# A graph layer in one kernel: each row's diagonal block formed last and stored once, with degrees subtracted, and ten pieces of A kept on chip

## The chip, the core and the metric

The kernel runs on one core of a Trainium2 chip. The core has five engines that run side by side, each with its own queue of instructions: TensorE (PE; its weight loads are listed apart as PEld), VectorE (DVE), ScalarE (ACT), GpSimd (POOL) and SyncE (SP), which here only issues transfers. Sixteen DMA engines move data between device memory and SBUF; a transfer is issued from the queue of SP, ACT or POOL. TensorE writes into PSUM, from which the other engines read. The metric is the device time of one execution in microseconds (us), as the median of several runs. All times below are from one profiled execution unless they are said to be runs.

## What is computed

With B = 8 graphs that share one adjacency of N = 4096 nodes, and F = FO = 256 features:

```python
def _L0_gnn_ref(H, W, A):
    HW = jnp.einsum('bnf,fo->bno', H, W)
    A_norm = jax.nn.relu((A + A.T) * 0.5)
    D = jnp.sum(A_norm, axis=1)
    D_safe = jnp.where(D > 0, D, 1.0)
    d_inv_sqrt = jnp.where(D > 0, D_safe ** (-0.5), 0.0)
    DAD = d_inv_sqrt[:, None] * A_norm * d_inv_sqrt[None, :]
    L_norm = jnp.eye(N, dtype=H.dtype) - DAD
    out = jnp.einsum('nm,bmo->bno', L_norm, HW)
    return jax.nn.relu(out)

x = _layernorm(x + _L0_gnn_ref(x, L0_gnn_W, adj), axis=-1)
```

The inputs are `x` (8, 4096, 256), `adj` (4096, 4096) and the 256 x 256 weights, all float32.

## The kernel before

**Algebra.** With r = d_inv_sqrt and e the degrees (1 where a degree is 0), row n of L_norm times HW is -r[n] times the sum over m of (A_norm - diag(e))[n, m] * r[m] * HW[m]. So the kernel forms A = A_norm and subtracts e from its diagonal, forms G = r * HW, multiplies, and scales with minus_r at the end.

**Stage 1, up to 585 us.** A is formed in 512 x 512 blocks, 8 rows of blocks by 8. For row i the loop takes the diagonal block (i, i) first and then, for j = i+1 to 7, the pair (i, j) and (j, i). One pass of the inner loop is called a step. In a step:

- `load_adj` brings the one or two blocks (1 MB each, SP's queue, 4 buffers `adj`).
- `symmetrise` transposes a block on PE (L515, 16 records a block, four PSUM buffers of the tag "b0") and VectorE adds the untransposed block into `sym` (L519, 4 additions a block; `sym` has 3 buffers).
- `beside` holds other work for PE in that step: first `multiply` for groups that are ready, then `form` for one new group of 128 nodes. `quota` gives one group to each pair step and to the diagonal steps of rows 4 to 7, none to the diagonal steps of rows 0 to 3.
- `keep` applies the relu with the factor one half (ACT, L523), takes sums over 32 columns (DVE, L526), marks which are used (POOL, L527), adds them up into `part` (L531) and stores the block to `a_dram` (1 MB, ACT's queue, L532). For a diagonal block POOL also copies its four 128 x 128 pieces on the diagonal into `diag` (L537).

When the last pair of row i is done, `degrees(i)` works out the row's e, r and minus_r from `part` (L543 to L547; the power is POOL's). `lower_diagonal` then subtracts e from the four pieces in `diag` (VectorE, L555) and stores each over its place in `a_dram` (POOL's queue, L558, 64 KB), behind the store of the whole block. `release_all(i)` calls it, after it has scaled the row's "held" groups.

`form(m)` transposes x of group m (L615), copies it from PSUM (ACT, L616), multiplies with the weights (L626), and evicts the 1 MB of G with the factor r (L636) to `g_dram` (L641). Groups 0 to 21 are formed when their r is known. The ten groups 22 to 31 are formed early and unscaled, held in SBUF, and scaled in `release` (L649, L651). In both cases `fetch(m)` brings a strip, A's rows of the group by its first 128 columns (64 KB from `a_dram`, POOL's queue, L574, 10 buffers), and `multiply` adds strip times G to `lead`, four PSUM banks that hold output block 0 for the length of stage 1 (L584).

Between the steps, `run_due` does pieces of another job, the lists of used columns. Two of its tiles, `hot` and `mixed`, sit in a `sym` and an `adj` buffer for some steps. Its last piece in a turn, `collect`, multiplies into `pl` on PE (L449), and `index` reads that on VectorE (L463 to L479).

**Stage 2** gathers the used columns of A and rows of G with indirect transfers on POOL's queue (L1031, L1039) and multiplies them (L1254) for the other 31 output blocks; VectorE and ScalarE finish each block with the residual and the normalisation. It reads `a_dram`, so it starts when the last store has landed; `lead` of the ten held groups runs before it on PE.

**Order.** Each engine works its queue in order. The order is made when the program is built, by a scheduler that takes instructions roughly in the order of the code, weighed by when their inputs are ready, and pools decide which earlier tile a new one waits for. Stores on ACT's queue stand between ACT's own instructions and wait there.

Of the kernel before, what the change touches and what calls it, by code (L numbers as in the profile page):

```python
# [9 lines left out]
F32 = mybir.dt.float32  # L10
AF = mybir.ActivationFunctionType
ALU = mybir.AluOpType
# [55 lines left out]
def kernel(  # L68
# [40 lines left out]
    HOLD = 10  # L109
# [36 lines left out]
    ident = const.tile([P, P], F32, name="ident")  # L146
# [12 lines left out]
    a_dram = dram.tile([N + 1, N], F32, name="a_dram")  # L159
# [66 lines left out]
    own = const.tile([P, NE, 2], F32, name="own")  # L226
# [263 lines left out]
    with (  # L490
# [9 lines left out]
        }  # L500
        strips = holds.enter_context(tc.tile_pool(name="strips", bufs=10))

# [18 lines left out]

        def keep(i, j, sym, diag):
            nc.scalar.activation(sym, sym, AF.Relu, scale=0.5)  # L523
            rows = slice(i * A, (i + 1) * A)
            sums = stat1.tile([P, A, S // E], F32, tag="sums", name=f"sums_{i}_{j}", bufs=3)
            nc.vector.tensor_reduce(sums, sym.rearrange("p a (c q) -> p a c q", q=E), AX.X, ALU.add)  # L526
            ins = nc.gpsimd.tensor_scalar(  # L527
                uses[:, rows, j * S // E : (j + 1) * S // E], sums, 0.0, None, ALU.is_gt
            )
            flags.append(ins.ins)  # L530
            nc.vector.tensor_reduce(part[:, rows, j], sums, AX.X, ALU.add)  # L531
            nc.scalar.dma_start(  # L532
                a_dram[i * S : (i + 1) * S, j * S : (j + 1) * S].rearrange("(a p) s -> p a s", p=P), sym
            )
            if i == j:
                for a in range(A):
                    nc.gpsimd.tensor_copy(diag[:, a, :], sym[:, a, a * P : (a + 1) * P])  # L537

# [9 lines left out]

        def lower_diagonal(i, diag):
            ms = slice(i * A, (i + 1) * A)  # L550
            minus_e = stat1.tile([P, A], F32, tag="minus_e", name=f"minus_e_{i}")
            nc.vector.tensor_scalar(minus_e, e[:, ms], -1.0, None, ALU.mult)
            for a in range(A):
                m = i * A + a
                nc.vector.scalar_tensor_tensor(  # L555
                    diag[:, a, :], ident, minus_e[:, a : a + 1], diag[:, a, :], ALU.mult, ALU.add
                )
                nc.gpsimd.dma_start(  # L558
                    a_dram[m * P : (m + 1) * P, m * P : (m + 1) * P], diag[:, a, :]
                )  # L560

# [14 lines left out]
        def fetch(m):  # L576

            t = strips.tile([P, P], F32, tag="strip", name=f"strip_{m}")
            load(t, a_dram[m * P : (m + 1) * P, :P])
            return t  # L580
# [73 lines left out]

        diags = {}

        def release_all(i):
            for m in range(i * A, (i + 1) * A):
                if m in held:
                    release(m)  # L660
            lower_diagonal(i, diags.pop(i))

# [55 lines left out]
        for i in range(NS):  # L718
            diag = stat1.tile([P, A, P], F32, tag="diag", name=f"diag_{i}")
            for j in range(i, NS):  # L720
                tij = load_adj(i, j)
# [24 lines left out]
                for (rows, cols, _, _), sym in parts:  # L746
                    keep(rows, cols, sym, diag)
                    run_due()
            degrees(i)
            diags[i] = diag  # L750
            if i != NS - 2:
# [221 lines left out]
    with (  # L973
# [292 lines left out]
        for q, (u, step) in enumerate(steps):  # L1266
            new = q == 0 or steps[q - 1][0] != u
            if new:
                prepare(u)
                after(4, classify, u)  # L1270
                rows = [2 * u + 1 + b for b in range(2)] if q > 0 and blocks(u) == 2 else []
# [33 lines left out]
            for c in range(NC):  # L1305
                for op in step:
                    rows = slice(0, P) if op[1] is None else slice(op[1] * L, (op[1] + 1) * L)
                    cols = slice(op[3] * E, (op[3] + op[4]) * E)
# [82 lines left out]
```

## Time and profile before

| | |
|---|---|
| runs | 1518.41 us median of 3 (1517.39 to 1519.67) |
| the profiled execution | 1526.28 us, span 1524.6 us, mean granted clock of TensorE 0.976 |
| traffic | 540.52 MB, mean 355 GB/s |
| stage 1 | 0 to about 585 us: `lead` of the held groups ends, `py` begins |
| stage 2 | 585 to 1524.6 us |

How to read the rows. A row of the page's groups has the line, engine, operation, tiles with the last loop numbers left out, and the count; behind the first bar the busy time in us and the mean of one in ns, behind the second the idle time of the engine just before, with what ended it. A row of the timeline has start, length, engine, line and tiles, "x4" for four instructions in a row, and in brackets the wait before the first of them with what ended it. A row of the windows has the window, its length, busy time and count for PE, PEld, DVE, ACT and POOL, then the granted clock, the DMA share and GB/s. The chain of waits is followed back from the end: start, length, what it was. A matmul of float32 shows as two records, so a group's four products into `lead` are eight.

### The profile page before, as it was taken

To read this page: it belongs to the slowest core of one execution; us is meant where nothing else is said; L and a number is where in the kernel's file an instruction comes from. 1 tells how busy PE (TensorE), PEld (TensorE's weight loads), DVE (VectorE), ACT (ScalarE), POOL (GpSimd) and SP (SyncE) were. 2 spreads that over 40 slices of the span, in tenths; PEclk is the share of its full clock that TensorE was granted. 3 is DMA by queue.
4 is the path that set the end of the run, shared out by engine and by line. 5 is a ranking of instruction groups with operands and counts; after the bars stand their busy time and mean duration, and the time that the engine had idled before them with its cause. 6 is when DMAs were issued, how large, how long until landed. Compare 5 with 4: busy or idle time off the path is not lost.

```text
span 1524.6 us, 20569 instructions
## 1 busy us (share of the span) xinstructions
PE 1430.9 (94%) x6768; PEld 759.5 (50%) x6768; DVE 1028.0 (67%) x3010; ACT 369.3 (24%) x462; POOL 744.7 (49%) x1547
## 2 busy tenths in 40 slices
PE   7999988989999999989999989998999999989996
PEld 6777867777777753333333333332333333333332
DVE  5677569789597726074757676886799149879544
ACT  4555544544455430000000101010100010101102
POOL 3444010012133327556667565576476635756663
PEclk9999999989999999999999989999999999999998
DMA  9999999998999999888989899999899969998996
GB/s 349 364 371 387 405 364 363 386 362 329 393 358 326 371 418 362 337 320 328 358 304 371 288 396 348 356 383 413 294 382 358 412 206 372 364 347 299 405 396 236
DMA packets 215264, 540.52 MB, mean 355 GB/s; under 512 B 17750, under 2 KB 107526, under 8 KB 180838
## 3 DMA queue, kind: packets, MB, share of 16 engines
q0 software_dynamic: 53808, 281.94, 48.1%
q1 hardware_dynamic: 93200, 126.62, 23.9%
q10 hardware_dynamic: 68144, 130.58, 22.5%
q8 instruction: 56, 0.92, 0.2%
q14 instruction: 56, 0.46, 0.1%
HBM read 425.72 MB, written 136.34 MB: 369 GB/s over the span
## 4 chain that ended last, share of the span: by engine, by line
PE 64%; DVE 14%; DMA 14%; issue 3%; ACT 2%; POOL 1%; another core or an unknown queue 1%; ACTq 0%; DVEq 0%; POOLq 0%
PE py L1254 46%; PE pg L626 8%; DMA a_dram<-sym 7%; PE lead L584 5%; DVE sym L519 4%; DMA xin<-in_x_dram 4%; DMA g<-g_dram,gi 2%; PE xtr L615 2%; PE tr L515 2%; ACT sym L523 1%; DVE sums L526 1%; DVE stats L806 1%; DVE xr L797 1%; PE lists L449 1%; DVE xr L830 1%
## 5 line engine op out<-in xcount | busy, mean ns | idle before, releaser
L1254 PE MATMUL py<-g,ga 128*32 128x512 f32 (+4 forms) x2880 | 651.4, 604 | 16.3 <-issue 11.4
L1254 PEld LDWEIGHTS py<-g,ga 128*32 128x32 f32 (+4 forms) x2880 | 230.5, 138 | 408.3 <-issue 389.8
L1039 POOL DMA_INDIRECT g<-g_dram,gi x256 | 288.9, 1128 | 164.3 <-issue 74.3
L1031 POOL DMA_INDIRECT ga<-a_dram,ai x256 | 271.7, 1061 | 159.4 <-issue 59.9
L787 ACT ACTIVATE y<-py,minus_r 128x512 f32<-128x512 f32 x120 | 81.0, 687 | 824.7 <-PE py L1254 598.8
L1254 PE MATMUL py<-g_hub,gh 128*128 128x512 f32 x496 | 234.5, 614 | 13.5 <-DVE low L464 6.6
L626 PE MATMUL pg<-w_sb,xt 128*128 128x256 f32 x1024 | 231.7, 385 | 7.9 <-ACT xt L616 7.7
L626 PEld LDWEIGHTS pg<-w_sb,xt 128*128 128x128 f32 x1024 | 195.8, 194 | 35.5 <-ACT xt L616 8.7
L519 DVE TENSOR_TENSOR sym<-tr,adj 128x512 f32<-128x512 f32 x256 | 162.2, 683 | 60.6 <-PE tr L515 51.1
L526 DVE TENSOR_REDUCE sums<-sym 128x64 f32<-128x2048 f32 x64 | 145.5, 2279 | 64.4 <-ACT sym L523 64.4
L1254 PEld LDWEIGHTS py<-g_hub,gh 128*128 128x128 f32 x496 | 92.3, 194 | 142.3 <-issue 127.2
L527 POOL TENSOR_SCALAR uses<-sums 128x64 uint8<-128x64 f32 x64 | 26.7, 417 | 268.4 <-DVE sums L526 234.9
L515 PE MATMUL tr<-ident,adj 128*128 128x128 f32 x1024 | 137.7, 282 | 19.2 <-DVE sym L519 14.0
L523 ACT ACTIVATE sym<-sym 128x2048 f32<-128x2048 f32 x64 | 122.7, 1918 | 122.4 <-DVE sym L519 118.3
L515 PEld LDWEIGHTS tr<-ident,adj 128*128 128x128 f32 x1024 | 115.6, 143 | 50.4 <-DVE sym L519 31.5
L241 DVE TENSOR_TENSOR_SCAN incl_r<-carry,lists 128x32 f32<-128x32 bf16 x13 | 2.9, 220 | 164.9 <-PE lists L396 164.9
L428 DVE TENSOR_TENSOR hot<-iota_q,at 128x1024 bf16<-128x1024 f32 x64 | 74.6, 1219 | 33.9 <-ACT y L787 32.1
L797 DVE TENSOR_TENSOR xr<-xr,y 128x2048 f32<-128x2048 f32 x31 | 70.8, 2284 | 38.9 <-ACT y L787 34.3
L615 PE MATMUL xtr<-ident,xin 128*128 128x128 f32 x512 | 71.9, 291 | 18.9 <-DVE sym L519 9.8
L830 DVE TENSOR_SCALAR xr<-xr,mv,root 128x256 f32<-128x256 f32 x248 | 84.3, 412 | 1.1
L806 DVE BATCH_NORM_STATS2 stats<-xr 128x6 f32<-128x256 f32 x248 | 84.0, 412 | 1.1
L584 PE MATMUL lead<-gt,strip 128*128 128x512 f32 x176 | 82.4, 593 | 0.0
(164 smaller groups left out, 1038.4 us busy)
## 6 DMA issues: line engine op xcount, KB each, us to landing
adj<-in_adj_dram SPq DMA_DIRECT2D x64, 1024.0 KB
a_dram<-sym ACTq DMA_DIRECT2D x64, 1024.0 KB
out_dram<-xr SPq DMA_DIRECT2D x31, 1024.0 KB
xr<-in_x_dram ACTq DMA_DIRECT2D x28, 1024.0 KB
xin<-in_x_dram SPq DMA_DIRECT2D x44, 512.0 KB
g_dram<-gt ACTq DMA_DIRECT2D x22, 1024.0 KB
xin<-in_x_dram POOLq DMA_DIRECT2D x20, 512.0 KB
g_dram<-held ACTq DMA_DIRECT2D x10, 1024.0 KB
```

The lines of the kernel that those rows point to most:

```text
L515: ins = nc.tensor.transpose(pt[:, c * P : (c + 1) * P], tji[:, c, a * P : (a + 1) * P], ident)
L519: nc.vector.tensor_add(sym[:, a, :], pt, tij[:, a, :])
L523: nc.scalar.activation(sym, sym, AF.Relu, scale=0.5)
L526: nc.vector.tensor_reduce(sums, sym.rearrange("p a (c q) -> p a c q", q=E), AX.X, ALU.add)
L584: nc.tensor.matmul(lead[c], lhsT=strip, rhs=g[:, c * S : (c + 1) * S], start=not done, stop=len(done) == NB - 1, skip_group_check=True,)
L615: nc.tensor.transpose(pt[:, k, c, :], xin[b // H][:, b % H + k, c * P : (c + 1) * P], ident)
L626: ins = nc.tensor.matmul(pg[:, k * FO : (k + 1) * FO], lhsT=xt[:, b + k, c, :], rhs=w_sb[:, c, :], start=(c == 0), stop=(c == FC - 1),)
L806: nc.vector.bn_stats(stats[:, b, :], z[:, b, :])
L830: nc.vector.tensor_scalar(z[:, b, :], z[:, b, :], mv[:, b, 0:1], rstd[:, b : b + 1], ALU.subtract, ALU.mult,)
L1031: nc.gpsimd.indirect_dma_start(out=at if both else at[:, : E if one else P], out_offset=None, in_=a_pairs if both else a_groups if one els ...
L1039: nc.gpsimd.indirect_dma_start(out=gt, out_offset=None, in_=g_dram, in_offset=bass.IndirectOffsetOnAxis(ap=gi[:, t : t + 1], axis=0), boun ...
L1254: return nc.tensor.matmul(py[2 * u + 1 + b][c][cols, :], lhsT=at[ps, off + cols.start : off + cols.stop], rhs=gt[ps, c * S : (c + 1) * S], ...
```

## The change

The loop over j goes from i+1 to 7 and then takes i: the diagonal block is the last step of its row, and the first step of row 0 is the pair (0,1), (1,0). In `keep` of a diagonal block `degrees(i)` and `lower_diagonal(i, sym)` are called ahead of the store, the subtraction works on `sym` itself, and the block is stored once. `diag`, its copies and its 32 stores of 64 KB are gone. For j = 0 POOL copies the first 128 columns of the rows of groups 22 to 31 from `sym` into a constant tile `kept`, and `fetch` hands these pieces out instead of loading a strip; the `strips` pool has 8 buffers instead of 10.

```diff
-        strips = holds.enter_context(tc.tile_pool(name="strips", bufs=10))
+        strips = holds.enter_context(tc.tile_pool(name="strips", bufs=8))
+        kept = holds.enter_context(tc.tile_pool(name="kept", bufs=1)).tile([P, HOLD, P], F32, name="kept")
...
-        def keep(i, j, sym, diag):
+        def keep(i, j, sym):
             nc.scalar.activation(sym, sym, AF.Relu, scale=0.5)
...
             nc.vector.tensor_reduce(part[:, rows, j], sums, AX.X, ALU.add)
+            if i == j:
+                degrees(i)
+                lower_diagonal(i, sym)
             nc.scalar.dma_start(
                 a_dram[i * S : (i + 1) * S, j * S : (j + 1) * S].rearrange("(a p) s -> p a s", p=P), sym
             )
-            if i == j:
-                for a in range(A):
-                    nc.gpsimd.tensor_copy(diag[:, a, :], sym[:, a, a * P : (a + 1) * P])
+            if j == 0:
+                for m in range(max(i * A, NB - HOLD), (i + 1) * A):
+                    nc.gpsimd.tensor_copy(kept[:, m - NB + HOLD, :], sym[:, m - i * A, :P])
...
-        def lower_diagonal(i, diag):
+        def lower_diagonal(i, sym):
...
-                m = i * A + a
-                nc.vector.scalar_tensor_tensor(
-                    diag[:, a, :], ident, minus_e[:, a : a + 1], diag[:, a, :], ALU.mult, ALU.add
-                )
-                nc.gpsimd.dma_start(
-                    a_dram[m * P : (m + 1) * P, m * P : (m + 1) * P], diag[:, a, :]
-                )
+                own = sym[:, a, a * P : (a + 1) * P]
+                nc.vector.scalar_tensor_tensor(own, ident, minus_e[:, a : a + 1], own, ALU.mult, ALU.add)
...
         def fetch(m):
 
+            if m >= NB - HOLD:
+                return kept[:, m - NB + HOLD, :]
             t = strips.tile([P, P], F32, tag="strip", name=f"strip_{m}")
...
         def release_all(i):
             for m in range(i * A, (i + 1) * A):
                 if m in held:
                     release(m)
-            lower_diagonal(i, diags.pop(i))
...
-            diag = stat1.tile([P, A, P], F32, tag="diag", name=f"diag_{i}")
-            for j in range(i, NS):
+            for j in (*range(i + 1, NS), i):
...
-                    keep(rows, cols, sym, diag)
+                    keep(rows, cols, sym)
                     run_due()
-            degrees(i)
-            diags[i] = diag
             if i != NS - 2:
                 release_all(i)
```

Both programs have the same number of instructions on PE (7580), ACT (750) and SP (1236); VectorE has 4 fewer (2811) and POOL 23 fewer (1182). Where they stand differs. In the rows below a tile's name ends in a running number, and `sym_1_2` is the tile of block (1,2).

ScalarE at the change from row 0 to row 1, before: the last store of row 0 is that of block (7,0), then comes the step of (1,1), then the pair (1,2), (2,1).

```order
L532 DMA a_dram_74<-sym_7_0_1626 128x4x512
L523 ACTIVATE sym_1_1_1849<-sym_1_1_1849 128x2048
L532 DMA a_dram_74<-sym_1_1_1849 128x4x512
L523 ACTIVATE sym_1_2_1924<-sym_1_2_1924 128x2048
L616 COPY xt_0_1978<-xtr_0_0_1979 128x512
L616 COPY xt_0_1978<-xtr_0_2_1985 128x512
L616 COPY xt_0_1978<-xtr_0_4_1991 128x512
L616 COPY xt_0_1978<-xtr_0_6_1997 128x512
L532 DMA a_dram_74<-sym_1_2_1924 128x4x512
```

The same place now:

```order
L536 DMA a_dram_74<-sym_7_0_1546 128x4x512
L524 ACTIVATE sym_0_0_1763<-sym_0_0_1763 128x2048
L524 ACTIVATE sym_1_2_1855<-sym_1_2_1855 128x2048
L536 DMA a_dram_74<-sym_1_2_1855 128x4x512
L617 COPY xt_0_1909<-xtr_0_0_1910 128x512
L617 COPY xt_0_1909<-xtr_0_2_1916 128x512
L617 COPY xt_0_1909<-xtr_0_4_1922 128x512
L617 COPY xt_0_1909<-xtr_0_6_1928 128x512
L524 ACTIVATE sym_2_1_1856<-sym_2_1_1856 128x2048
L536 DMA a_dram_74<-sym_0_0_1763 128x4x512
```

The diagonal block's store followed its relu at once; now it stands behind the relus of (1,2) and (2,1), a store and four copies, and waits for the subtraction.

VectorE at the change from row 3 to row 4, before: the sums of the last block of row 3, (7,3), and the step of (4,4), with the reading of `pl` between.

```order
L526 TENSOR_REDUCE sums_7_3_4074<-sym_7_3_3954 128x64
L531 TENSOR_REDUCE part_68<-sums_7_3_4074 128x4
L463 TENSOR_SCALAR low_1_4112<-pl_1_4079 128x22
L464 SCALAR_TENSOR_TENSOR low_1_4112<-pl_1_4079,low_1_4112 128x22
L519 TENSOR_TENSOR sym_4_4_4143<-tr_4_4_0_4144,adj_4_4_4141 128x512
L466 CAST gi_1_4115<-low_1_4112 128x22
L475 SCALAR_TENSOR_TENSOR ai_1_4117<-low_1_4112,group_of_116 128x12
L479 TENSOR_SCALAR ai_1_4117<-low_1_4112 128x1 x3
L479 TENSOR_SCALAR ai_1_4117<-low_1_4112 128x7
L519 TENSOR_TENSOR sym_4_4_4143<-tr_4_4_1_4150,adj_4_4_4141 128x512
```

The same place now, between the first and the second addition of the pair (4,5):

```order
L520 TENSOR_TENSOR sym_4_5_4126<-tr_4_5_0_4128,adj_4_5_4122 128x512
L548 TENSOR_SCALAR none_3_4065<-deg_3_4064 128x4
L466 CAST gi_1_4114<-low_1_4111 128x22
L475 SCALAR_TENSOR_TENSOR ai_1_4116<-low_1_4111,group_of_116 128x12
L549 TENSOR_TENSOR e_71<-deg_3_4064,none_3_4065 128x4
L479 TENSOR_SCALAR ai_1_4116<-low_1_4111 128x1 x2
L556 TENSOR_SCALAR minus_e_3_4071<-e_71 128x4
L479 TENSOR_SCALAR ai_1_4116<-low_1_4111 128x1
L551 TENSOR_SCALAR minus_r_73<-r_72 128x4
L559 SCALAR_TENSOR_TENSOR sym_3_3_4030<-ident_60,minus_e_3_4071,sym_3_3_4030 128x128 x4
L479 TENSOR_SCALAR ai_1_4116<-low_1_4111 128x7
L520 TENSOR_TENSOR sym_4_5_4126<-tr_4_5_1_4134,adj_4_5_4122 128x512
```

The degrees of row 3 and the subtraction from (3,3) now stand ahead of the second addition of (4,5); they stood ahead of (4,4) before.

TensorE at the same change, before: the last product into `pl`, the step of (4,4) with its `lead`, and the form of group 12.

```order
L449 MATMUL pl_1_4079<-mixed_1_3422,hot_1_3421 128x44
L515 MATMUL tr_4_4_0_4144<-ident_60,adj_4_4_4141 128x128 x4
L515 MATMUL tr_4_4_1_4150<-ident_60,adj_4_4_4141 128x128 x4
L515 MATMUL tr_4_4_2_4156<-ident_60,adj_4_4_4141 128x128 x4
L515 MATMUL tr_4_4_3_4162<-ident_60,adj_4_4_4141 128x128 x4
L584 MATMUL lead_0_177<-gt_11_4036,strip_11_4062 128x512
L584 MATMUL lead_1_178<-gt_11_4036,strip_11_4062 128x512
L584 MATMUL lead_2_179<-gt_11_4036,strip_11_4062 128x512
L584 MATMUL lead_3_180<-gt_11_4036,strip_11_4062 128x512
L615 MATMUL xtr_12_0_4177<-ident_60,xin_12_0_4172 128x128 x4
```

The same place now:

```order
L449 MATMUL pl_1_4078<-mixed_1_3409,hot_1_3408 128x44
L516 MATMUL tr_4_5_0_4128<-ident_60,adj_5_4_4124 128x128 x4
L516 MATMUL tr_4_5_1_4134<-ident_60,adj_5_4_4124 128x128 x4
L516 MATMUL tr_4_5_2_4140<-ident_60,adj_5_4_4124 128x128 x4
L516 MATMUL tr_4_5_3_4146<-ident_60,adj_5_4_4124 128x128 x4
L516 MATMUL tr_5_4_0_4152<-ident_60,adj_4_5_4122 128x128 x4
L516 MATMUL tr_5_4_1_4158<-ident_60,adj_4_5_4122 128x128 x4
L516 MATMUL tr_5_4_2_4164<-ident_60,adj_4_5_4122 128x128 x4
L516 MATMUL tr_5_4_3_4170<-ident_60,adj_4_5_4122 128x128 x4
L616 MATMUL xtr_12_0_4181<-ident_60,xin_12_0_4176 128x128 x4
```

The diagonal step ahead of `pl` is now that of (3,3), with its `lead` and no form; behind `pl` stand the 32 transposes of a pair, and the form of group 12 behind these.

More of the change, by code (lines that the diff above doesn't have):

```diff
@@ L653, in release @@
             waiting.append((m, g, fetch(m)))
-        diags = {}
         def release_all(i):
```

## Prediction

> **What bounds the kernel now.** I read the page first, then the waits and the chain of stage 1 (up to 585 us, where `form`, `symmetrise` and `lead` end), then the timeline at the ends of the rows.
>
> ```profile
> span 1524.6 us, 20569 instructions
> PE 1430.9 (94%) x6768; PEld 759.5 (50%) x6768; DVE 1028.0 (67%) x3010; ACT 369.3 (24%) x462; POOL 744.7 (49%) x1547
> ...
> 0.00:585.00 585.00, 538.94 (x2896) 419.41 (x2897) 402.36 (x769) 280.88 (x330) 154.45 (x982) 0.98 1.00 370
> ```
>
> The last row is stage 1: its length, the busy time of PE, PEld, DVE, ACT and POOL, the clock, the DMA share and GB/s. PE is idle for 585.0 - 538.9 = 46.1 us; everything that this change can win in stage 1 by a shorter wait is within these 46 us. The DMA share is 1.00 as well, so two things stand near their limit. The edit does not touch PE's own work: the same transposes and products in both kernels. What it can do is to move PE's idle time. Who ends it:
>
> ```profile
> PE tr L515 <- DVE sym L519: 14.0, 19, 4.0
> PE xtr L615 <- DVE sym L519: 9.8, 8, 2.1
> PE xtr L615 <- DMA xin<-in_x_dram: 8.7, 2, 6.1
> ...
> PE tr L515 <- DMA adj<-in_adj_dram: 4.3, 1, 4.3
> ...
> DVE sym L519 <- DMA a_dram<-sym: 5.8, 5, 1.8
> ...
> POOL strip L574 <- DMA a_dram<-diag: 3.3, 1, 3.3
> ```
>
> The columns are total, times, longest. More than half of PE's idle time, 23.8 us, is the wait for VectorE's addition `sym`: the four "b0" buffers in PSUM are full until it has read them. The waits that the edit removes by name are small: the strip's wait for the diagonals' stores is 3.3 us in all, on POOL. The chain says what stands behind VectorE in row 0:
>
> ```profile
> 56.54 8.96 DMA a_dram<-sym
> ...
> 70.46 8.96 DMA a_dram<-sym
> ...
> 84.53 11.72 DMA a_dram<-sym
> ...
> 113.37 10.07 DMA a_dram<-sym
> ```
>
> A 1 MB store of A lands 9 to 12 us after its issue and frees one of three `sym` buffers; from 56.54 to 70.46 one step of row 0 takes 13.9 us, of which 9.0 are this landing. So in row 0 the pace is the recycling of `sym`; later rows follow PE.
>
> **The change part by part.** What it removes is cheap where it stands:
>
> ```profile
> L558 POOL DMA_DIRECT2D a_dram<-diag x32 | 20.5, 645 | 10.6 <-DMA a_dram<-sym 6.5 <-DVE diag L555 3.9
> L574 POOL DMA_DIRECT2D strip<-a_dram x32 | 17.8, 559 | 12.8 <-PE lead L584 8.9 <-DMA a_dram<-diag 3.3 <-DMA xin<-in_x_dram 0.4
> L537 POOL COPY diag<-sym 128x128 f32<-128x128 f32 x32 | 8.5, 304 | 41.8 <-ACT sym L523 41.8
> q0 software_dynamic: 512, 1.05, 2.8%
> ```
>
> 32 diagonal stores x 0.645 us, 10 of the 32 strip loads x 0.559 and 32 copies x 0.304 come to 20.6 + 5.6 + 9.7 = 35.9 us of POOL; 10 copies into `kept` come back (3.0 us). POOL is busy 154 of 585 us, and PE's list of waits above has no POOL in it: **0**. Without that cover the 3.0 us would be the price. As traffic: the last row is the window from 100 to 200 us, in which 4 diagonal stores and 12 strips (16 x 64 KB) took 2.8% of 100 us of all 16 engines, 0.175 us each. 42 such transfers go, 7.35 us. That is the most they can give, if every microsecond of stage 1 were DMA's; the least is 0. In rows 1 to 7 PE sets the pace and only 5.8 + 4.3 us of waits name a store or an `adj` load, so I take **-2**.
>
> What it moves is the formless step. `quota` gives the diagonal steps of rows 0 to 3 no group to form, so PE has only 16 transposes and a `lead` of 3.4 us (8 of the 80 records that take 34.33 us, below) in them, while VectorE, ScalarE and the stores have a full block. Before, these four steps stand at the start and at the changes of row 0 to 1, 1 to 2, 2 to 3; after, at 0 to 1, 1 to 2, 2 to 3, 3 to 4.
>
> *The start* loses its formless step:
>
> ```profile
> 16.77 6.23 PE L515 MATMUL tr<-ident,adj 128*128 128x128 f32 x48
> 25.13 2.41 PE L615 MATMUL xtr<-ident,xin 128*128 128x128 f32 x16 [2.13 <-DVE sym L519]
> ```
>
> Block (0,0) is 16 of these 48 transposes, 2.1 us, and the wait of 2.13 behind them is VectorE, which has (0,0)'s four additions to do first. Both gone is -4.2; 0 if row 0's store loop takes it back. The loop begins with the first pair's store, which moves ahead with the pair: **-3.5**.
>
> *0 to 1.* The store of (0,0) now stands on ScalarE behind two relus of the next step and four copies, and its `sym` buffer is the one that (3,1) takes.
>
> ```profile
> 132.98 0.37 ACTq L532 DMA_DIRECT2D a_dram<-sym  x1
> ...
> 141.17 0.68 DVE L519 TENSOR_TENSOR sym<-tr,adj 128x512 f32<-128x512 f32 x1
> ```
>
> The store at this place of the queue goes out at 132.98 before; one relu more and the subtraction make it about 136. With the 10.07 us of the chain's row it lands at 146. (3,1)'s first addition is the fifth from 141.17, at some 143.6: 2.4 us late, and 5.2 where the wait for POOL shown next, 2.75, comes on top. Queued behind it on VectorE are three additions and the next sums; PE waits for the additions, with a `lead` beside. Bounds 0 and +5.2, taken **+2**, near the lower count less a little cover.
>
> *1 to 2 and 2 to 3.* There is a formless step in both kernels. What is new is that the degrees and the subtraction stand ahead of a store, where they stood beside it. What they take, at the end of row 0:
>
> ```profile
> 115.29 0.87 DVE L544 TENSOR_SCALAR none<-deg 128x4 f32<-128x4 f32 x1
> ...
> 119.31 0.17 DVE L547 TENSOR_SCALAR minus_r<-r 128x4 f32<-128x4 f32 x1 [2.75 <-POOL r L546]
> 119.39 1.13 DVE L555 SCALAR_TENSOR_TENSOR diag<-ident,minus_e,diag 128x128 f32<-128x128 f32 x4
> ```
>
> From the first to the end of the last 5.2 us, 2.75 of them waiting for POOL's power. At these two places VectorE paid them before too, so 0 is one end; a store that is 5.2 us later and meets no cover is the other, 5.2 each. The `lead` of 3.4 us beside the step covers most: **+1** each, +2.
>
> *3 to 4* becomes formless. The nearest rows are those of (3,3) before, at 2 to 3, then those of (4,4), which has a form:
>
> ```profile
> 300.08 1.91 PE L515 MATMUL tr<-ident,adj 128*128 128x128 f32 x16
> 306.31 3.12 PE L515 MATMUL tr<-ident,adj 128*128 128x128 f32 x16 [4.32 <-DMA adj<-in_adj_dram]
> 310.08 1.11 PE L515 MATMUL tr<-ident,adj 128*128 128x128 f32 x4 [0.65 <-DVE sym L519]
> 311.73 1.97 PE L515 MATMUL tr<-ident,adj 128*128 128x128 f32 x8 [0.54 <-DVE sym L519]
> 315.12 1.12 PE L515 MATMUL tr<-ident,adj 128*128 128x128 f32 x4 [1.42 <-DVE sym L519]
> ...
> 389.59 7.17 PE L626 MATMUL pg<-w_sb,xt 128*128 128x256 f32 x32 [1.08 <-ACT xt L616]
> ```
>
> The waits in brackets add to 4.32 + 0.65 + 0.54 + 1.42 = 6.9 us; at 3 to 4 before, 1.08. The difference is 5.8. By hand: after (3,3)'s last addition come its relu and sums,
>
> ```profile
> L526 DVE TENSOR_REDUCE sums<-sym 128x64 f32<-128x2048 f32 x64 | 145.5, 2279 | 64.4 <-ACT sym L523 64.4
> ...
> L523 ACT ACTIVATE sym<-sym 128x2048 f32<-128x2048 f32 x64 | 122.7, 1918 | 122.4 <-DVE sym L519 118.3
> ...
> L449 PE MATMUL pl<-mixed,hot 128*128 128x44 bf16 (+1 forms) x64 | 1.9, 180 | 0.0
> ```
>
> 1.92 + 2.28, then one addition (0.68), the 5.2 of above, and the next addition (0.68), in this order on VectorE: 10.8 us, during which PE has 3.4 of `lead`, 32 of the 64 `pl` (1.0) and the 16 transposes (1.9) that fit in "b0", 6.3. The wait is 4.5, near the 5.8, which I take: **+5.8** (bounds 0 and 6.9).
>
> *Rows 4 to 7* have a form of 6.9 us in their diagonal step, which covers the later store: 0; the price without that cover is a rival below.
>
> *The end.* (7,7) is last in both kernels, but its store now waits for the degrees and, on ScalarE, for three evictions and a `held` scaling.
>
> ```profile
> 544.75 0.38 ACTq L532 DMA_DIRECT2D a_dram<-sym  x1
> ...
> 555.54 2.23 POOL L558 DMA_DIRECT2D a_dram<-diag  x4 [6.50 <-DMA a_dram<-sym]
> ...
> 564.89 1.07 POOL L1031 DMA_INDIRECT ga<-a_dram,ai  x1 [0.68 <-issue]
> ...
> 550.36 34.33 PE lead L584 x80
> ```
>
> Before, A is whole only when the four diagonals behind 555.54 have landed. After, the store goes at about 552 and lands some 11 us later, 563, close to where the gathers began; `lead` keeps PE busy until 584.7: 0. Past about 20 us of delay it would cost one for one. Stage 2 keeps its code: 0.
>
> Sum: -2 - 3.5 + 2 + 2 + 5.8 = +4.3. It is made against the profiled run, 1526.28 us (span 1524.6), which lies 7.87 above the median of the runs, 1518.41; 1530.6 there, **1522.7** against the median.
>
> **Rivals.**
>
> (a) *DMA is the bound.* For it: the share of 1.00. Against it: the share of 1.00 goes with 370 GB/s over the stage and shares of 1.02 and 1.06 with 390 and 405 in the windows under (c), so a full share is not a full rate; and PE's waits hardly name DMA. If true, the bubbles fall into time in which the queues catch up, and all traffic removed counts: the 42 transfers' 7.35, with the start's gain between 0 and 3.5: 1518.4 - 7.35 = 1511 (down to 1507.6; up to 1515 where only half of the traffic counts). Faster.
>
> (b) *Cover takes all.* The `lead` beside each diagonal step and the buffers absorb the later stores, and 3 to 4 costs no more than the start gave: 1518.4 within 3. This is also the time if the change does not do what it says, with the strip path never on PE's way, as the 3.3 us say.
>
> (c) *The clock falls behind the new bubble* (slower). Its place is 3 to 4; it decides from a single wait of about 4 us. In the traces:
>
> ```profile
> 220.00:240.00 20.00, 15.41 (x91) 12.91 (x90) 17.69 (x36) 10.56 (x11) 4.09 (x11) 0.91 0.92 323
> 300.00:320.00 20.00, 13.08 (x67) 11.14 (x66) 18.24 (x29) 7.49 (x7) 5.55 (x13) 0.68 1.02 390
> 310.00:315.00 5.00, 3.08 (x12) 2.28 (x12) 5.00 (x10) 0.03 (x1) 3.62 (x9) 0.50 1.06 405
> ```
>
> Behind the wait of 4.32 the granted clock goes to 0.50; 20 us x (1 - 0.68) = 6.4 us of clock are lost there, 1.8 in the window of 220 to 240. If PE needs that time, it is 4.3 + 1.8 to 4.3 + 6.4: 1524.5 to 1529, named 1528. The Trainium skill, "TensorE: Matmul & The Clock Gate", section "HAM oscillation — how this bites in real kernels", has this as a rule: no idle gaps of TensorE over some 3.4 us, or it comes back at half clock. The 0.50 agrees with it; by the rule the 4.5 to 5.8 us at 3 to 4 would be such a gap, and the time would be (c)'s. Against (c): after a gap VectorE is behind as well, and a slow PE then waits less.
>
> (d) *The later store stalls every row.* The diagonal's store is 5.2 us late at each of rows 4 to 7 too, form or not: 4 x 5.2 us more, 1543.5. Only row 0 is paced by stores in the chain, which speaks against it.
>
> **How the numbers follow.** The sum as it stands, 1519.5 to 1526, 0.40 (0.12 of it within 0.2%); (a) 0.25; (b) 0.15, of which 0.02 faster; (c) 0.14; (d) 0.06. About 0.2% (3 us) is what a measurement of this kernel tells from no change. Faster 0.27, same 0.12 + 0.13 = 0.25, slower 0.28 + 0.14 + 0.06 = 0.48. The range goes from (a)'s low side, about 1508, to (c)'s upper end with 0 to 1 at its bound of +5.2, 1518.4 + 4.3 + 6.4 + 3.2, about 1532; it leaves out (d) and little else.
>
> **What would show it.** Right: row 0's second step begins about 3.5 us earlier; `sym` of (3,1) waits some 4 us for a store near 141; PE idle 5 to 6 us between 385 and 400 behind `sym`; the waits of 2 to 3 stay; `lead` to `py` without a gap. Wrong: DMA share under 0.95 in rows 1 to 7 with PE's idle under 46 us in stage 1 (then (a)); a clock of 0.5 behind 3 to 4 (then (c)); waits of `sym` for `a_dram` at rows 5 to 7 (then (d)); a gap ahead of `py`.

## Result: slower by 0.94%, and the profile after

| | before | changed |
|---|---|---|
| median of 4 runs | 1518.73 us | 1533.37 us |
| ratio of the runs, 95% interval | | 1.0094 (1.0077 to 1.0112) |
| profiled execution, span | 1524.6 us | 1529.1 us |
| stage 1 ends (first `py`) | 584.53 us | 597.26 us |
| traffic | 540.52 MB | 537.77 MB |

The forecast was +4.3 us and a range up to 1532; the runs say +14.6. The two spans differ by 4.5 us only, but that is chance: the profiled execution of before lay 7.9 us above its median, and what it has more stands in stage 2, 940.1 us against 931.8 (in the second pair of traces below stage 2 took 885.8 and 885.3). Stage 1, which the edit touches, ends 12.7 us later, and this is what has to be explained.

The page of the changed kernel, its span and busy times, and the window of stage 1's first 585 us:

```profile
span 1529.1 us, 20466 instructions
PE 1431.5 (94%) x6768; PEld 757.0 (50%) x6768; DVE 1026.3 (67%) x3010; ACT 367.7 (24%) x462; POOL 719.1 (47%) x1483
...
0.00:585.00 585.00, 530.80 (x2866) 412.44 (x2867) 401.18 (x768) 277.32 (x326) 112.74 (x909) 0.97 0.97 357
```

POOL gave back its work about as counted: up to the end of stage 1 it is busy 122.3 us instead of 154.0, 31.7 less where the prediction counted 35.9 - 3.0 = 32.9. Over the whole span POOL has 64 instructions fewer in the trace (1547 and 1483), and VectorE as many (3010). The DMA share fell to 0.97 and the clock by 0.01; PE is busy 8.1 us less in the same 585 us. The list of waits up to 590 us (who waited for what: total, times, longest) has a new row:

```profile
PE tr L516 <- DVE sym L520: 18.4, 20, 4.6
...
DVE sym L520 <- DMA a_dram<-sym: 12.1, 4, 8.9
...
PE lead L585 <- DMA strip<-a_dram: 7.3, 1, 7.3
POOL strip L573 <- DMA a_dram<-sym: 6.5, 1, 6.5
```

Before, `lead` waited for nothing. Now its first product waits 7.3 us for a strip. The chain of waits at the change from row 0 to row 1:

```profile
130.13 1.07 DVE sym L559 x4
...
131.21 8.88 DMA a_dram<-sym
...
140.39 5.74 DMA strip<-a_dram
...
146.17 6.49 PE lead L585 x8
```

The windows of the same place; the granted clock is the third figure from the end:

```profile
140.00:145.00 5.00, 0.00 (x0) 0.00 (x0) 4.80 (x6) 0.12 (x1) 4.58 (x8) 0.66 1.03 413
145.00:150.00 5.00, 3.83 (x5) 1.76 (x6) 0.10 (x1) 0.00 (x0) 0.00 (x0) 0.50 1.04 392
...
390.00:395.00 5.00, 2.31 (x15) 1.72 (x13) 4.11 (x13) 0.90 (x1) 0.95 (x1) 0.92 1.04 401
395.00:400.00 5.00, 5.00 (x28) 4.77 (x27) 3.87 (x5) 3.26 (x5) 2.53 (x4) 0.74 1.04 358
```

The subtraction ends, the block (0,0) is stored and lands 8.9 us later, POOL then issues eight strips, and 5.7 us after that group 0's strip is there. Behind the wait the clock is at 0.50, and eight records of `lead` take 6.49 us where eight take 3.43 at full clock (8 of the 80 in 34.33 us): another 3.06. The last two rows are the place where the clock was expected to fall, behind rows 3 to 4: there it went to 0.92 and 0.74, a loss of 5 x 0.08 + 5 x 0.26 = 1.7 us. The Trainium skill, "TensorE: Matmul & The Clock Gate", section "HAM oscillation — how this bites in real kernels", has half clock behind idle gaps over some 3.4 us; the 0.50 behind a wait of 7.29 agrees with it. But the clock also fell where no wait was that long: `kept12` (below) had 0.73 from 125 to 130 us, behind a wait of 2.13.

Where stage 1 fell behind is seen from the time at which ScalarE copies the first piece of each group's transposed x (first `xt<-xtr` of a group, us). Two more executions are beside it, `before_again` and `changed_again` (below), on two other chips, on which the kernel before ran at 1468.8 and 1469.6 us:

| group, step in the changed kernel | before | changed | difference | before_again | changed_again | difference |
|---|---|---|---|---|---|---|
| 29, last pair of row 0 | 112.0 | 107.4 | -4.6 | 113.1 | 106.4 | -6.7 |
| 0, first pair of row 1 | 131.2 | 126.3 | -4.9 | 132.2 | 124.5 | -7.7 |
| 1, second pair | 147.2 | 153.1 | +5.9 | 148.2 | 151.8 | +3.6 |
| 30, fifth pair | 194.3 | 200.4 | +6.1 | 195.3 | 198.8 | +3.5 |
| 4, first pair of row 2 | 235.5 | 234.4 | -1.1 | 233.3 | 232.3 | -1.0 |
| 11, last pair of row 3 | 372.6 | 372.5 | -0.1 | 369.4 | 371.1 | +1.7 |
| 15, end of row 4 | 438.7 | 444.4 | +5.7 | 435.3 | 443.0 | +7.7 |
| 18, end of row 5 | 488.6 | 498.7 | +10.1 | 484.1 | 497.6 | +13.5 |
| 21, (7,7) | 540.9 | 553.6 | +12.7 | 536.5 | 552.5 | +16.0 |

From group 29 to group 11 the changed kernel has one diagonal block less behind it (16 transposes, 1.9 us); at 15, 18 and 21 both have done the same. So: some 3 to 6 us won at the start, about 11 lost between groups 0 and 1, 4.5 to 7 won back up to row 2, some 4 lost between rows 3 and 4 (5.8 to 6.0 less the 1.9), 4.4 to 5.8 in row 5, 2.6 after it.

Row 5 in the changed kernel: ScalarE's queue, VectorE and PE, from the timeline.

```profile
481.41 0.37 ACTq L536 DMA_DIRECT2D a_dram<-sym  x1
...
491.70 1.89 DVE L520 TENSOR_TENSOR sym<-tr,adj 128x512 f32<-128x512 f32 x3 [8.87 <-DMA a_dram<-sym]
...
492.44 0.66 PE L516 MATMUL tr<-ident,adj 128*128 128x128 f32 x4 [4.64 <-DVE sym L520]
492.94 5.30 PE L585 MATMUL lead<-gt,strip 128*128 128x512 f32 x8
```

The store issued at 481.41 is that of block (5,7). VectorE's first addition of (5,5) waits 8.87 us for its landing, PE 4.64 us behind VectorE, and the next `lead` is slow again (5.30). And rows 3 to 4 on PE and VectorE, with the end of stage 1 from the chain:

```profile
371.79 2.45 PE L616 MATMUL xtr<-ident,xin 128*128 128x128 f32 x16 [1.40 <-DVE sym L520]
...
388.93 1.31 PE L516 MATMUL tr<-ident,adj 128*128 128x128 f32 x8 [0.31 <-DVE deg L547]
391.06 1.14 DVE L559 SCALAR_TENSOR_TENSOR sym<-ident,minus_e,sym 128x128 f32<-128x128 f32 x4
392.19 4.27 DVE L520 TENSOR_TENSOR sym<-tr,adj 128x512 f32<-128x512 f32 x7
...
392.93 2.31 PE L516 MATMUL tr<-ident,adj 128*128 128x128 f32 x12 [2.69 <-DVE sym L520]
...
563.09 34.33 PE lead L585 x80
```

PE's wait of 2.69 ends when VectorE, after the degrees and the subtraction from (3,3), comes to the second addition of (4,5) at 392.19. At the end `lead` covers the last store as before: `py` follows without a gap.

### The profile page after: what moved, and what is told of

Its sections match the earlier page's. It is cut to its first block, busy times and chain, and to the rows that moved or that the text cites. A ratio compares the mean times of both kernels' runs of the same rounds, so it can differ in the third digit from the quotient of the medians.

```text
span 1529.1 us, 20466 instructions
## 1 busy us (share of the span) xinstructions
PE 1431.5 (94%) x6768; PEld 757.0 (50%) x6768; DVE 1026.3 (67%) x3010; ACT 367.7 (24%) x462; POOL 719.1 (47%) x1483
## 2 busy tenths in 40 slices
DMA packets 213920, 537.77 MB, mean 352 GB/s; under 512 B 17078, under 2 KB 106854, under 8 KB 179494
## 4 chain that ended last, share of the span: by engine, by line
PE 69%; DVE 13%; DMA 9%; issue 4%; ACT 3%; POOL 1%; ACTq 0%; DVEq 0%; POOLq 0%
PE py L1249 49%; PE pg L627 7%; DMA a_dram<-sym 6%; PE lead L585 6%; PE tr L516 3%; DVE sym L520 3%; DVE sums L527 3%; PE xtr L616 2%; DMA g<-g_dram,gi 2%; ACT sym L524 1%; ACT xt L617 1%; PE lists L449 1%; DVE stats L801 1%; DMA gh<-a_dram 1%; DVE xr L825 1%
## 5 line engine op out<-in xcount | busy, mean ns | idle before, releaser
L1026 POOL DMA_INDIRECT ga<-a_dram,ai x256 | 279.4, 1091 | 144.9 <-issue 59.0
L1249 PE MATMUL py<-g_hub,gh 128*128 128x512 f32 x496 | 231.4, 608 | 7.1 <-issue 5.8
L617 ACT COPY xt<-xtr 128x512 f32<-128x512 f32 x128 | 68.5, 593 | 107.7 <-PE xtr L616 106.0
L585 PE MATMUL lead<-gt,strip 128*128 128x512 f32 x176 | 87.1, 622 | 7.3 <-DMA strip<-a_dram 7.3
```

What stands on the lines that cost most here:

```text
L585: nc.tensor.matmul(lead[c], lhsT=strip, rhs=g[:, c * S : (c + 1) * S], start=not done, stop=len(done) == NB - 1, skip_group_check=True,)
L617: nc.scalar.copy(xt[:, b : b + 2], pt)
L1026: nc.gpsimd.indirect_dma_start(out=at if both else at[:, : E if one else P], out_offset=None, in_=a_pairs if both else a_groups if one els ...
L1249: return nc.tensor.matmul(py[2 * u + 1 + b][c][cols, :], lhsT=at[ps, off + cols.start : off + cols.stop], rhs=gt[ps, c * S : (c + 1) * S], ...
```

## Experiments

Each kernel is compared with the kernel before on its own chip, whose median was 1508.7 us for 1 to 3, 1469.6 for 4 to 7, 1468.8 for 8 to 11, and 1507.5 for 12 and 13. Ratios are to that, with the 95% interval. The expectations of 1 to 3 are in us of the first chip, where the kernel before took 1518.7, so they are compared as ratios. In the diffs "..." stands for lines left out.

**1. `kept12`: the strips of groups 0 and 1 stay on chip too.**

```diff
-        strips = holds.enter_context(tc.tile_pool(name="strips", bufs=8))
-        kept = holds.enter_context(tc.tile_pool(name="kept", bufs=1)).tile([P, HOLD, P], F32, name="kept")
+        strips = holds.enter_context(tc.tile_pool(name="strips", bufs=6))
+        kept = holds.enter_context(tc.tile_pool(name="kept", bufs=1)).tile([P, HOLD + 2, P], F32, name="kept")
...
-            if m >= NB - HOLD:
+            if m < 2 or m >= NB - HOLD:
...
```

> The changed kernel, but groups 0 and 1 also get their strip from SBUF (12 pieces in kept, strips with 6 buffers). Theory (strip): after the change the first lead product waits for the strip of group 0, which waits for the single late store of block (0,0); that is 7.3 us of idle TensorE and about 3 us of half clock behind it. Then this kernel has no lead wait near 146 us, a clock of 1.0 there, and is 9 to 11 us faster than the changed kernel: 1522.5 to 1524.5 us. Rival (sym buffer): the same late store holds the sym buffer of (3,1), so VectorE and with it TensorE wait there anyway: less than 4 us faster, 1529.5 us or more.

Measured: 1512.05 us, ratio 1.0031 (1.0008 to 1.0054); stage 1 ends at 590.05. The timeline of PE at row 0 to 1:

```profile
137.44 1.02 PE L586 MATMUL lead<-gt,kept 128*128 128x512 f32 x2
138.30 3.23 PE L516 MATMUL tr<-ident,adj 128*128 128x128 f32 x28
141.37 2.74 PE L586 MATMUL lead<-gt,kept 128*128 128x512 f32 x6
...
484.85 1.11 PE L516 MATMUL tr<-ident,adj 128*128 128x128 f32 x4 [4.65 <-DVE sym L520]
```

The additions of (3,1) in the same trace, and two windows (the clock is the third figure from the end):

```profile
141.36 2.48 DVE L520 TENSOR_TENSOR sym<-tr,adj 128x512 f32<-128x512 f32 x4 [0.54 <-DMA a_dram<-sym]
...
125.00:130.00 5.00, 3.68 (x18) 3.08 (x19) 5.00 (x10) 2.44 (x5) 3.66 (x46) 0.73 0.98 294
130.00:135.00 5.00, 5.00 (x23) 4.33 (x22) 4.38 (x10) 3.44 (x4) 2.60 (x40) 0.92 1.06 398
```

No wait at `lead`, and group 1 begins at 144.6 instead of 153.1. Stage 1 is 7.2 us shorter than the changed kernel's, and the ratio 0.6% smaller, 9.5 us: the strip it was. Without it the difference to the first trace of before goes from -4.2 at group 0 to -2.6 at group 1. This +1.6 is not the `sym` buffer of (3,1): VectorE waits 0.54 us for that and PE not at all. It is the clock, which was 1.00 in both windows before: 5 x 0.27 + 5 x 0.08 = 1.75 us. In the three later traces with the same row 0 to 1 and no half clock there (`hot_late`, `spread25`, `hot_late_both`) the difference grows by 0.3 to 0.5. The wait in row 5 is unmoved.

**2. `order_alone`: only the order of the blocks is changed; the separate subtraction, its 64 KB stores and all 32 strips stay.**

```diff
-            for j in range(i, NS):
+            for j in (*range(i + 1, NS), i):
```

> The kernel before with the diagonal step last in its row, but with its separate subtraction and 64 KB stores, all 32 strips and no kept. Theory (strip): the block's store leaves at once after its relu and the degrees are not ahead of the additions of the next pair, so neither the wait at 0 to 1 nor that at 3 to 4 appears in full; the start is some 4 us earlier: 1516 to 1522 us. Rival (moved formless step): the order itself costs, whatever the store does: 1528 us or more, with idle TensorE at 0 to 1 and 3 to 4 as in the changed kernel.

Measured: 1522.09 us, ratio 1.0094 (1.0063 to 1.0124); stage 1 ends at 591.69. The theory's 1516 to 1522 is a ratio of 0.998 to 1.002, the rival's 1528 one of 1.006: my theory fell here, the order alone costs. POOL and PE at row 0 to 1, and VectorE and PE at rows 3 to 4:

```profile
130.96 2.44 POOL L558 DMA_DIRECT2D a_dram<-diag  x4
136.50 4.30 POOL L574 DMA_DIRECT2D strip<-a_dram  x8 [3.10 <-DMA a_dram<-diag]
...
142.82 3.78 PE L584 MATMUL lead<-gt,strip 128*128 128x512 f32 x4 [5.47 <-DMA strip<-a_dram]
...
381.61 0.69 DVE L519 TENSOR_TENSOR sym<-tr,adj 128x512 f32<-128x512 f32 x1 [7.08 <-issue]
382.35 1.10 PE L515 MATMUL tr<-ident,adj 128*128 128x128 f32 x4 [4.43 <-DVE sym L519]
```

The block leaves at once, but the degrees come only after the last block of the row, whatever the store does, and the strips wait for the four diagonal pieces. In the kernel before these pieces went out at 120.04; here at 130.96, and PE comes to `lead` at 137.35, 4.0 us earlier than before. So it is the order that takes the slack from the strip: between groups 0 and 1 this kernel loses 9.5 us to the first trace of before, the changed kernel 10.8, and storing once adds about 2 us to the wait (7.3 against 5.5). At rows 3 to 4 PE waits too, but at another place, in the step of (3,3): VectorE begins (3,3)'s additions 7.08 us late, and the profile names no cause. The runs of this kernel spread from 1513.7 to 1530.6.

**3. `row0_first`: the changed kernel, but row 0 as before** (diagonal first, four separate stores; `kept` holds the last six groups).

```diff
-            for j in (*range(i + 1, NS), i):
+            for j in (*range(i + 1, NS), i) if i > 0 else range(NS):
...
```

> The changed kernel, but row 0 keeps its diagonal block first with the separate subtraction and the four 64 KB stores (kept holds the last 6 groups). Theory (strip): the 10.6 us lost between rows 0 and 1 are gone, and so are the 4 to 5 us won at the start: 1533.4 - 10.6 + 4.7 = about 1527.5 us; what is left over the kernel before, about 9 us, is that of rows 3 to 5. Rival (later rows cost nothing, all of the loss is row 0's): 1518 to 1521 us. Rival (sym buffers in later rows carry the whole loss): 1533 us.

Measured: 1511.03 us, ratio 1.0022 (0.9995 to 1.0049); stage 1 ends at 589.07. The theory's 1527.5 is a ratio of 1.006 and lies outside the interval; the rival's 1518 to 1521 (1.000 to 1.002) lies inside it. I left out that with row 0's diagonal first and row 1's last no diagonal step stands at the change of row 0 to 1 at all: group 0 begins 4.2 us earlier there than before, so about as much as the start had gained is gained here instead. The later rows do cost, against the rival's reason: row 5's wait is left (5.20 us at 483.68) and the 2.68 us at rows 3 to 4.

**4. `changed_again`: the changed kernel on the chip of the next three.**

> The changed kernel once more, on the chip of the other three of this call. Both theories: a ratio of 1.008 to 1.011 to the kernel before, lead's first product waiting 6 to 8 us for a strip near 140 us.

Measured: 1486.65 us, ratio 1.0126 (1.0107 to 1.0144), a little above the expected; `lead` waits 7.56 us at 144.66.

**5. `hot_late`: `kept12` with the list pieces behind row 4 due five blocks later.**

```diff
-                at = 4 if i == 2 else 0
+                at = 4 if i == 2 else 5
```

> kept12 (ratio 1.0031 to the kernel before) with the list pieces behind row 4 due five blocks later, so that hot takes its sym buffer after row 5 and not in it. Theory (two buffers): block (5,5) waits because hot leaves only two sym buffers and (5,5) needs that of (5,7), whose store has just been issued; the 4.65 us of idle TensorE near 485 us and the half clock behind it go: 4 to 7 us less than kept12, a ratio of 0.998 to 1.000, unless row 6 pays it. Rival (late diagonal store): the wait comes from the diagonal's later store and stays: 1.002 to 1.004.

Measured: 1467.79 us, ratio 0.9989 (0.9976 to 1.0003); stage 1 ends at 582.77, 7.3 us before `kept12`'s. PE in the step of (5,5):

```profile
476.51 1.91 PE L516 MATMUL tr<-ident,adj 128*128 128x128 f32 x16
478.26 3.60 PE L586 MATMUL lead<-gt,strip 128*128 128x512 f32 x8
```

The transposes and the `lead` of (5,5) run without a wait, and from group 15 to 18 this kernel wins 3.9 us on the first trace of before, where `kept12` loses 4.8. In row 5 `hot` had held one of three `sym` buffers; a pair takes the other two, and a single block behind a pair then waits for the pair's first store. The edit also takes the list's own work on VectorE and PE out of row 5; that the buffer is what counts is read from the wait of 8.87 us, which names the store. The old order pays for row 5 too, though less (9 below).

**6. `spread25`: `kept12` with the pair step that has no group moved from (2,7) to (2,5).**

```diff
-            return int(j > i or i > 3)
+            return int((j > i or i > 3) and (i, j) != (2, 5))
```

> kept12 with the pair step of row 2 that has no group moved from (2,7) to (2,5), so that it no longer stands beside the formless step of (2,2). Theory (formless steps side by side): the 5.3 + 2.6 + 0.7 us of idle TensorE near 300 to 310 us shrink to under 3 and the clock there stays over 0.9: 5 to 8 us less than kept12, a ratio of 0.998 to 1.000. Rival (the adj loads or VectorE have no slack in row 2 anyway): the wait moves to (2,5) and the ratio stays at 1.002 to 1.004.

Measured: 1481.37 us, ratio 1.0077 (1.0058 to 1.0095). The wait went to (2,5), as the rival had it, from the timeline of PE:

```profile
268.30 1.12 PE L516 MATMUL tr<-ident,adj 128*128 128x128 f32 x4 [4.58 <-DVE sym L520]
273.45 3.68 PE L617 MATMUL xtr<-ident,xin 128*128 128x128 f32 x16 [4.04 <-DVE sym L520]
```

But the ratio is above what either side expected. Stage 1 ends 3.4 us later than `kept12`'s; `kept12` was not run on this chip, so how much of the rest is the chip stays open.

**7. `form33`: `kept12` with one group moved from (3,5) to (3,3).**

```diff
-            if i in (2, 3) and j == i:
-                return 0
-            return int(j > i or i > 3)
+            if i in (2, 3) and j == i:
+                return int(i == 3)
+            return int((j > i or i > 3) and (i, j) != (3, 5))
```

> kept12 with one group moved from the pair step (3,5) to the diagonal step (3,3). Theory (a diagonal step without a form at 3 to 4 is what costs there): the waits of 1.40 and 2.69 us near 363 and 385 us go and nothing of their size comes at (3,5): 3 to 6 us less than kept12, a ratio of 0.999 to 1.001. Rival (degrees ahead of the additions cost whatever TensorE has beside, or (3,5) pays the same): 1.002 to 1.004.

Measured: 1480.15 us, ratio 1.0087 (1.0052 to 1.0123). The waits at 363 and 385 are gone, as the theory had it, and (3,5) pays for them, as the rival had it:

```profile
335.69 1.12 PE L516 MATMUL tr<-ident,adj 128*128 128x128 f32 x4 [4.67 <-DVE sym L520]
...
354.12 0.21 PE L395 MATMUL pr<-rest,ones 128*128 128x32 bf16 x1 [2.90 <-DVE rest L390]
```

The second wait is for the list's work. Again the ratio is above both expectations, with stage 1 ending 1.5 us later than `kept12`'s. So moving a step without a group moves PE's waits along with it, 4.1 us at (3,3), 6.1 and more at (3,5), 8.6 at (2,5), and neither of the two places tried is cheaper. No run gave that step a group without taking one from another.

**8. `before_again`: the kernel before, traced beside the next three.**

> The kernel before, for a trace on the same chip as the other three. Both theories: stage 1 ends within 1.5 us of the 584.5 us of the first trace.

Stage 1 ended at 580.13, 4.4 us before the first trace: an execution's stage 1 varies by more than I had allowed.

**9. `before_hot_late`: the kernel before with the edit of 5 alone.**

> The kernel before with only the list pieces behind row 4 due five blocks later (hot after row 5). Theory (two buffers hurt where a diagonal step is last): before, (5,5) comes first in its row and asks for one buffer while every pair has a group beside it, so little is to be won: a ratio of 0.998 to 1.001. Rival (two buffers cost any order the same): 0.994 to 0.996, stage 1 shorter by 6 to 8 us.

Measured: 1470.51 us, ratio 1.0022 (1.0001 to 1.0044), a little above the expected. Row 5 does get shorter: from group 15 to 18 this kernel wins 3.2 us on `before_again` and 4.3 on the first trace of before. Waits like this one of the first trace are gone:

```profile
456.07 7.17 PE L626 MATMUL pg<-w_sb,xt 128*128 128x256 f32 x32 [1.76 <-ACT xt L616]
```

So the list's work in row 5 costs the old order 3 to 4 us there as well, where the new order pays 8.7 (`hot_late` against `kept12`). The difference, 4.4 to 5.5, is about what the change lost in row 5. Rows 6 and 7 give part of it back: stage 1 ends only 2.0 us earlier (578.11). Stage 2 begins with a new wait; that it comes of the list being read later is likely, but was not tried:

```profile
586.15 5.29 PE L1254 MATMUL py<-g,ga 128*32 128x512 f32 x26 [2.66 <-DMA g<-g_dram,gi]
```

**10. `changed_hot_late`: the changed kernel with the edit of 5 alone.**

> The changed kernel with only the list pieces behind row 4 due later; the strip wait near 140 us stays. Theory (two separate causes that add): stage 1 is 6.5 to 8.5 us shorter than the changed kernel's 597 us, and the ratio to the kernel before falls from 1.009 to 1.013 to 1.004 to 1.008. Rival (the later waits are slack behind the first): stage 1 shortens by less than 3 us, 1.008 or more.

Measured: 1479.03 us, ratio 1.0068 (1.0049 to 1.0088). The ratio is within what two causes that add should give, but its interval reaches the rival's 1.008, and stage 1 ends at 593.23, only 3.0 us before `changed_again`'s where 6.5 to 8.5 were expected. What speaks for adding is row 5: from group 17 to 18 the difference to the first trace of before falls by 3.9 us (8.1 to 4.2), where it grew by 3.5 in `changed_again` (5.6 to 9.1). This execution was 3.7 us behind `changed_again` at group 0 already (128.2 against 124.5), ahead of anything that the edit moves. The strip's wait is untouched:

```profile
147.91 6.71 PE L585 MATMUL lead<-gt,strip 128*128 128x512 f32 x8 [6.85 <-DMA strip<-a_dram]
```

**11. `hot_late_both`: `hot_late` with the other use of `hot` moved from row 3 to row 4** (`at = 10 if i == 2 else 5`).

> hot_late (strips of groups 0 and 1 on chip, hot after row 5) with the other use of hot also moved, from row 3 to row 4. Theory: the reading of pl leaves the formless step of (3,3), the waits of 1.83, 1.40 and 2.69 us near 339 to 385 us shrink by half or more, and pair steps of row 4 with a group beside them hide the missing buffer: 2 to 5 us less than hot_late, a ratio of 0.995 to 0.998. Rival (row 4's pairs stop for the buffer instead): 0.999 to 1.003.

Measured: 1472.23 us, ratio 1.0022 (1.0004 to 1.0040): the rival. Row 4 waits for the buffer and for the list's work:

```profile
386.30 1.12 PE L617 MATMUL xtr<-ident,xin 128*128 128x128 f32 x4 [4.70 <-DVE sym L520]
...
402.72 1.10 PE L516 MATMUL tr<-ident,adj 128*128 128x128 f32 x8 [2.49 <-DVE pos_k L245]
```

**12. `hot_split`: `hot_late` with that use one block earlier** (`at = 3 if i == 2 else 5`), which also puts the additions of (4,5) ahead of row 3's degrees in VectorE's queue.

> hot_late with the other use of hot, in row 3, one block earlier, so that pl is multiplied beside (7,3) and not between (3,3) and (4,5); in VectorE's queue the additions of (4,5) then stand ahead of row 3's degrees. Theory (pl and the degrees ahead of the additions make the wait at 3 to 4): the waits of 1.40 and 2.69 us near 363 and 385 us shrink to under 2 together and group 12 begins 3 to 5 us earlier than in hot_late, ratio 0.995 to 0.998. Rival (the formless step itself makes it): the waits stay at 3 us or more in sum, ratio 0.998 to 1.001.

Measured: 1511.04 us, ratio 1.0037 (1.0016 to 1.0057), above both. PE in row 3, then VectorE and PE at rows 3 to 4:

```profile
340.86 2.82 PE L516 MATMUL tr<-ident,adj 128*128 128x128 f32 x12 [3.24 <-DVE sym L520]
...
387.26 2.29 DVE L527 TENSOR_REDUCE sums<-sym 128x64 f32<-128x2048 f32 x1 [2.06 <-ACT sym L524]
389.47 0.68 DVE L520 TENSOR_TENSOR sym<-tr,adj 128x512 f32<-128x512 f32 x1
...
390.20 3.38 PE L516 MATMUL tr<-ident,adj 128*128 128x128 f32 x16 [2.91 <-DVE sym L520]
```

The wait at rows 3 to 4 stays, 2.91 us in one piece, near the rival's 3, though the degrees now stand behind the first two additions: it is the sums of (3,3), and the relu that they wait for, that hold up the first addition of (4,5) now. From group 11 to 12 this kernel loses 6.8 us, `hot_late_again` 7.5. What the move cost besides came in row 3.

**13. `hot_late_again`: `hot_late` on the chip of 12.**

> hot_late once more beside hot_split, on its chip. Both theories: a ratio of 0.997 to 1.001 to the kernel before; waits of about 1.4 and 2.7 us near 363 and 385 us.

Measured: 1504.87 us, ratio 0.9981 (0.9959 to 1.0003). In both runs of this kernel the ratio lies 0.1 to 0.2% under 1, and in both the interval reaches 1. No version here is shown to beat the kernel before.

## Why the prediction was wrong

**The bound, right.** Stage 1 moved, by PE's idle time and clock: up to its end PE is idle 54.2 us instead of 46.1, and busy 543.1 instead of 538.4 with the same work. Stage 2's code and the tail did not move.

**The start, right.** -3.5 was forecast; the traces show -4.6 and -6.7 at the end of row 0, of which 1.9 is work put off: 2.7 and 4.8 won.

**0 to 1, wrong, and the main miss.** The step said +2 with a bound of +5.2, and it is 11. I followed the late store to the `sym` buffer of (3,1) and priced that. VectorE does wait for this buffer (2.00 us in the changed kernel, from 138.17, until the store has landed at 140.09), but where the strip does not stop PE, PE does not wait for it: 0.3 to 0.5 us were lost there instead of 2. The same store also releases the strips, and the strips release `lead`, which stands in PE's queue ahead of everything else. In (b) I set the strip path aside with "the strip path never on PE's way, as the 3.3 us say". These 3.3 us were POOL's wait in the order of before, where the strips were issued at 125.81 and `lead` came at 141.38: with the 5.7 us that the strips take, some 10 us of slack. Now they are issued at 140.39, 14.6 us later, and PE is at `lead` 2.5 us earlier: 7.3 us of waiting, and 3.1 of half clock behind it. The two rows of the kernel before:

```profile
125.81 4.32 POOL L574 DMA_DIRECT2D strip<-a_dram  x8 [3.32 <-DMA a_dram<-diag]
...
141.38 1.88 PE L584 MATMUL lead<-gt,strip 128*128 128x512 f32 x4
```

So a term that stood in the sum at nothing, the strip's path to `lead`, was the largest one. A short wait off the path says nothing about the slack behind it. `kept12` shows the cause, `order_alone` that the order and not the single store takes most of it (9.5 us).

**The clock, right as a mechanism, and mostly in another place.** (c) had it behind rows 3 to 4, where it is 1.7 us in this trace; behind the strip's wait it is 3.06.

**1 to 2 and 2 to 3, wrong in sign for the first.** +2 in sum was forecast; up to group 4 the changed kernel wins 4.5 to 7.2, in `kept12` 7.5, and loses 1.0 to 2.7 up to group 11. Of the 7.2 and 7.5 some 3 us are the first trace of before itself, which `before_again` passes 3.2 us faster. The wait for `xin` at 197.31 (2.64, in `before_again` 1.08) is gone and that for VectorE at 232.41 (4.04) is 2.14; the list's pieces behind row 1 now run beside a pair instead of the diagonal block. That this is why was not tried by itself.

**3 to 4, near in size, its reason only in part.** +5.8 was forecast, and it is 4 at equal work. The account by hand put the degrees and the subtraction ahead of the additions, and in the changed kernel PE's 2.69 us end just behind them. But with them behind the first additions (`hot_split`) PE waits 2.91 for the sums of (3,3) instead, so they are not what makes it slow. The step without a group is the likelier cause, since its waits go where it goes (`form33`, `spread25`); shown it is not, as each of these runs took the group from another step.

**Rows 4 to 7, wrong.** Priced 0, it is 4.4 to 5.8 in row 5 and 2.6 after. Rival (d) had the wait, in four rows and from the late store of the diagonal. It came in one row, from `hot`, which I knew to sit in a `sym` buffer there and left out of the count. `hot_late` takes it away, and more, since the list's work cost the old order 3 to 4 us there too. The 2.6 us at the end stay open.

**The traffic, open.** -2 was taken of 0 to 7.35 us. No run has the traffic alone; the share fell from 1.00 to 0.97 while PE's waits rose, so the gain that (a) promised did not come.

**The removed work on POOL, right:** 31.7 us less busy in stage 1 against 32.9 counted, and no one waited for it.

## What to carry to other kernels

When a store is moved, list everyone who reads what it frees or writes, the buffer's next owner and the loads from memory behind it, and follow each to the engine whose queue it stops; a wait that is short today is no measure of the slack behind it. A pool's real depth is what its other users leave, step by step: three buffers were two in the row where the new order needed three. And less traffic, or less work on an engine that nobody waits for, bought nothing here that the runs show.

## What the runs showed of the hardware that was not expected

Eight strips of 64 KB issued in a row took 5.74 us from the first issue until the product that needed the first of them could run, with 4.59 us of issuing on POOL; store and strip together made 15.0 us from a finished tile (131.21) to its first use (146.17). After a wait of 7.29 us eight products ran at half clock (6.49 us for 3.43), and in `kept12` the clock was 0.73 from 125 to 130 us behind no wait over 2.13 us, though in `hot_late` it stayed at 1.00 there behind a wait of 2.14. The same kernel ran at 1469, 1508 and 1519 us on different chips, with the change at 1.0094 and 1.0126 of it on two of them.
